# First group's softmax weights begun after half of its maxima, and q/k projections of the first batch placed between its up and down pieces

## The chip, the cores and the metric

The kernel runs on one core of one Trainium2 chip. The metric is the device time of one execution in microseconds. Engines are called as in the profile: PE (TensorE, with its weight loads PEld), DVE (VectorE), ACT (ScalarE), POOL (GpSimd) and SP (SyncE, here only an issuer of DMAs).

## The reference

A gated transformer block on x of shape 8 x 1024 x 256. Everything starts from the normalised input; attention and a feed-forward gate are multiplied and added to x.

```python
xn = _layernorm(x)
q, k, v = split(xn @ W_attn + b_attn)        # 16 heads of 16
q, k = _apply_rope(q), _apply_rope(k)
att = softmax(where(causal, q @ k.T / sqrt(16), -inf))
s = (att @ v) @ W_proj + b_proj
h = silu(xn @ (w_gate/127).T) * (xn @ (w_up/127).T)   # 768 hidden
g = silu(h @ (w_down/127).T)
out = x + s * g
```

## The kernel before

**Groups and steps.** The work is cut into 8 batches of 4 groups; a group is 4 heads of one batch. Queries and keys are halves of 512 and tiles of 128. For every group two things are done on the scores.

*Maxima.* `Group.maxima` (L499) computes scores with queries on the partitions, into one of three PSUM tiles `pm`, and DVE reduces them: `top_far` (L513) for keys of the first half seen by queries of the second, `trash`/`top` (L515) for the half on the diagonal. `maxima_units` lists 38 such units per group: 11 for the first half of the queries and 27 for the second (16 far ones of 512 columns, 11 on the diagonal). The maxima of one half are then split in two on POOL (`shift_parts`, L527), transposed on PE, copied to `rows` on ACT and written by two DMAs on SP into two rows of `q_st` (`shift_queries`, L537).

*Weights.* `Group.weights` (L552) computes the scores again with keys on the partitions into `pw`, now with the shift included through those rows of `q_st`, and ACT takes the exponential (L569). POOL clears the part above the diagonal (L576). `values` (L590) multiplies by v into `av`. There are 12 steps `n` per group (4 for the first half of the queries, 8 for the second) and 4 slots per step.

**The pipeline.** `attention` (L660) runs the weights of one group and, dealt over its 48 slots by `quarter_steps`, the maxima of the next group. In each slot, `slot` also runs pieces from one long list `chain`: projections of q, k and v (`project_qk`, `project_v`), the up pieces (`hidden`) and down pieces (`down`) of the feed-forward, output projections and transposes. The list is run by a pace: so much of it per slot that it ends with the batch. All instructions are in the order of the program on each engine; `manual_schedule` leaves it alone.

**The opening.** The first group has no group before it, so its maxima stand alone ahead of the first `attention`, with one piece of the chain after every other unit:

```python
for n, unit in enumerate(units):
    first.maxima(*unit)
    cast()
    if n % 2:
        run(1)
    if n in (8, 11, 14, 17):
        ...
        groups[1].load(which % 2, which // 2)
```

**q and k through DRAM.** `project_qk` leaves a pair `high`, `low` in SBUF (two buffers each), and SP stores both to a DRAM tensor `qk` (L254, 256 KB each). `Group.load` (L477) reads them back per group, head by head, into `q_st` and `k_st`: for each of q and k and each half four DMAs of 128 KB, each into 16 partitions (L483). All of these, the input x of the next batch (L87) and the rows of the shift (L544) go through SP's one queue in the order of the program.

**The lists.** For the first batch the chain begins with `qk[4:]` (q and k of the heads of groups 2 and 3), `v[2:]` and the 12 up pieces of the first quarter, then the 4 down pieces of that quarter. A down piece needs all gated products `h_high`, `h_low` that POOL makes from the up pieces.

Of the kernel before, what the change touches and what calls it, by code (L numbers as in the profile page):

```python
# [35 lines left out]
def gated_block_kernel(ctx: ExitStack, tc: tile.TileContext, x, wqk, wv, bv, wp, bp, wg, wu, wd, rope, out):  # L36
# [7 lines left out]
    QT = HALF // P  # L44
# [19 lines left out]
    def flush(keep=0):  # L64
        while len(later) > keep:
            later.pop(0)()

    def cast(keep=0):
        while len(casts) > keep:
            casts.pop(0)()  # L70
# [556 lines left out]
    STEPS = 3 * QT  # L627
# [3 lines left out]
    def add_values(count):  # L631
        for _ in range(count):
            of, half, kb, es = waiting.pop(0)
            ending = of.values(half, kb, es)
            if ending:
                endings.append(ending)

    def streams(columns, passes=1):
        return columns * passes / 2.4e3

    def quarter_steps(group, after):

        units = after.maxima_units() if after else []

        costs = [sum(0.2 + n / 960 for _ in heads) for _, heads, _, n in units]
        total, spent = sum(costs), 0.0
        plan = []
        for half, kb in group.weight_steps():
            columns = HALF - max(0, kb * P - half * HALF)
            for i in range(4):  # L650
                here = []
                while units and spent * 4 * STEPS < (len(plan) + 0.5) * total:
                    here.append(units.pop(0))
                    spent += costs.pop(0)
                weights = columns if 2 * columns > HALF else 2 * columns * (1 - i % 2)
                maxima = sum(len(heads) * max(n, 256) for _, heads, _, n in here)
                plan.append((streams(weights), streams(maxima), here))
        return plan

    def attention(groups, at, plan, slot, vector):  # L660

        group = groups[at]
        after = groups[at + 1] if at + 1 < len(groups) else None
        loaded = groups[at + 2] if at + 2 < len(groups) else None
        plan = iter(plan)
        for n, (half, kb) in enumerate(group.weight_steps()):
            es = []
            for pair in range(2):
                e, banks = group.weights(half, kb, pair)
                es.append(e)  # L670
                for second, bank in enumerate(banks):
                    weights, maxima, units = next(plan)
                    if bank:
                        bank()
                    cast()
                    slot(weights)
                    if pair == 0 and second and n == 2:
                        group.shift_queries(1)
                    if pair == 0 and second and n == QT + 3 and after:
                        after.shift_queries(0)  # L680
                    if pair == 1 and second and endings:
                        endings.pop(0)()
                    for unit in units:
                        after.maxima(*unit)
                    if not units:
                        flush()
                    slot(maxima)
                if vector:
                    vector.pop(0)()
            waiting.append((group, half, kb, es))  # L690
            if len(waiting) == 3:
                add_values(2)
            for entry in delayed:
                entry[0] -= 1
            while delayed and delayed[0][0] <= 0:
                delayed.pop(0)[1]()
            if n == QT - 1 and after:
                after.shift_parts(0)
            if n == STEPS - 1 and after:
                after.shift_parts(1)  # L700
            if loaded:
                if n == QT - 1:
                    loaded.load(0, 0)
                elif n == 2 * QT - 1:
                    loaded.load(1, 0)
                elif n == STEPS - 1:
                    loaded.load(0, 1)
                    loaded.load(1, 1)
# [14 lines left out]
    def forward(exact, general=None):  # L723
# [3 lines left out]
        groups = [None] * (NB * GROUPS)  # L727
# [12 lines left out]
        def by(count, pieces):  # L740
            return [pieces[i : i + count] for i in range(0, len(pieces), count)]

        def mixed(*kinds):
            both = [((i + 0.5) / len(x), p) for x in kinds for i, p in enumerate(x)]
            return [piece for _, pieces in sorted(both, key=lambda entry: entry[0]) for piece in pieces]

        qk, v = batches[0].project_in()
        chain = sum(qk[4:] + v[2:], [])
        aside = []
        marks = {}  # L750
        for b in range(NB):
            batches[b].weights, batches[b].general = weights, general
            last = b + 1 == NB

            outs = [[p[:1], p[1:]] for p in map(batches[b - 1].project, range(NT // 2))] if b else [[[], []]] * (NT // 2)
            (u0, d0), (u1, d1), (u2, d2), (u3, d3) = batches[b].feed_forward()
            (t0, o0), (t1, o1), (t2, o2), (t3, o3) = outs
            first = mixed(by(2, u0), aside)
            chain += first[:-2] + t0 + first[-2:]
            marks[b] = len(chain)  # L760

            if last:
                chain += o0 + d0[:2] + t1 + o1 + t2 + d0[2:] + o2 + t3 + u1
            else:
                chain += o0 + d0[:2] + t1 + d0[2:] + o1 + u1[:4] + t2 + u1[4:6] + o2 + u1[6:10] + t3 + u1[10:]
            chain += o3 + d1 + u2
            if last:
                chain += d2[:2] + u3[:6] + d2[2:] + u3[6:] + d3
                continue
            after = batches[b + 1]  # L770
            qk, v = after.project_in()
            if exact:
                chain += after.open() + d2 + mixed(by(2, u3), qk[:4]) + qk[4] + mixed(by(1, d3), by(1, after.splits()))
                aside = qk[5:] + v
            else:
                chain += d2 + u3 + after.open() + sum(qk[:4], []) + d3 + sum(qk[4:] + v, [])
# [13 lines left out]
        first = groups[0]  # L790
        for _, piece in batches[0].splits():
            piece()
        units = first.maxima_units()
        early = sum(qt < QT for qt, *_ in units)
        for n, unit in enumerate(units):
            first.maxima(*unit)
            cast()
            if n % 2:
                run(1)
            if n in (8, 11, 14, 17):  # L800
                which = (8, 11, 14, 17).index(n)
                groups[1].load(which % 2, which // 2)
            if n == early - 1:
                first.shift_parts(0)
            if n == early + 6:
                first.shift_queries(0)
        flush()
        first.shift_parts(1)
        for t in (wp_sb, bp_sb):
            nc.vector.tensor_scalar(t, t, QSCALE / 2, None, ALU.mult)  # L810

        for b in range(NB):

            here = range(b * GROUPS, (b + 1) * GROUPS)
            for i in here:
                open_group(groups, batches, i + 2)
            plans = [quarter_steps(groups[i], groups[i + 1] if i + 1 < len(groups) else None) for i in here]
            total = sum(w + m for plan in plans for w, m, _ in plan) + sum(us for us, _ in chain[done[0] : marks[b + 1]])
            slots = 2 * sum(len(plan) for plan in plans)
            due, spent, at = [0.0], [0.0], [0]  # L820
            vectors = []

            def slot(before):
                due[0] += total / slots
                spent[0] += before
                at[0] += 1
                while (
                    done[0] < (marks[b + 1] if b + 1 < NB or batches[b].complete[0] == GROUPS else marks[b + 1] - 6)
                    and spent[0] + chain[done[0]][0] / 2 <= due[0]
                ):  # L830
                    spent[0] += chain[done[0]][0]
                    run(1)
                if at[0] == 8 and b < NB - 1:
                    if b:
                        load_x(b + 1)
                    vectors.extend([lambda: None] * 5 + norm_steps(b + 1))

            for i, plan in zip(here, plans):
                attention(groups, i, plan, slot, vectors)
                groups[i] = None  # L840
            run(marks[b + 1] - done[0])
        while waiting:
# [12 lines left out]
    with tc.tile_pool(name="setup", bufs=1) as sp:  # L855
# [62 lines left out]
        early = Group(opening, 0)  # L918
        qk, v = opening.project_in()
# [82 lines left out]
```

## Time and profile before

| | us |
|---|---|
| median of 3 runs | 1567.24 (1566.38 to 1567.66) |
| the profiled execution | 1564.28 |
| its span | 1562.5 |
| busy of PE in the span | 1506.6 |
| busy of DVE | 1083.7 |
| busy of ACT | 958.6 |
| busy of POOL | 740.4 |
| mean granted PE clock | 0.994 |

The start of the profiled execution, as it stands in the timeline: the first maximum of the first group begins at 42.0 us, its first weights at 77.6 us; the last of its own maxima ends on DVE at 79.3 us; the first down piece begins at 85.0 us; the second group's weights begin at 129.0 us.

A page row of an engine gives busy time, its share of the span and the number of instructions. The slices cut the span in 40 parts of 39 us, and each digit is a busy share in tenths. In a list of waits the numbers are the total in us, how often, and the longest. In the windows an engine's number is its busy time in the stretch, with the count of its instructions in brackets; after the engines come the granted PE clock, the mean busy share of the 16 DMA engines, and GB/s. PE's busy time counts overlapping instructions once and includes their latency, so a busy PE is not a PE at full speed.

### The profile page before, as it was taken

To read this page: it belongs to the slowest core of one execution; us is meant where nothing else is said; L and a number is where in the kernel's file an instruction comes from. 1 tells how busy PE (TensorE), PEld (TensorE's weight loads), DVE (VectorE), ACT (ScalarE), POOL (GpSimd) and SP (SyncE) were. 2 spreads that over 40 slices of the span, in tenths; PEclk is the share of its full clock that TensorE was granted. 3 is DMA by queue.
4 is the path that set the end of the run, shared out by engine and by line. 5 is a ranking of instruction groups with operands and counts; after the bars stand their busy time and mean duration, and the time that the engine had idled before them with its cause. 6 is when DMAs were issued, how large, how long until landed. Compare 5 with 4: busy or idle time off the path is not lost.

```text
span 1562.5 us, 29525 instructions
## 1 busy us (share of the span) xinstructions
PE 1506.6 (96%) x9801; PEld 1057.9 (68%) x9801; DVE 1083.7 (69%) x3284; ACT 958.6 (61%) x2076; POOL 740.4 (47%) x1443
## 2 busy tenths in 40 slices
PE   5899999999999999999999999999999999999997
PEld 2567667776677766777667766777667776666664
DVE  6776766767767677776677766776776767777642
ACT  2157665676657666566665766667665766656664
POOL 4455443653436444464434734365353644434353
PEclk9899999999999999999999999999999999999999
DMA  6912544444554254643455454354454525445301
GB/s 178 193 29 42 110 96 62 96 63 96 110 96 75 36 123 91 107 72 59 100 86 105 66 96 96 70 101 63 95 110 89 82 37 123 84 75 83 49 16 44
DMA packets 92085, 132.86 MB, mean 85 GB/s; under 512 B 13713, under 2 KB 41873, under 8 KB 91922
## 3 DMA queue, kind: packets, MB, share of 16 engines
q1 hardware_dynamic: 90944, 129.82, 44.3%
q8 instruction: 80, 1.31, 0.4%
q10 hardware_dynamic: 978, 1.05, 0.3%
q14 instruction: 83, 0.68, 0.2%
HBM read 87.82 MB, written 41.94 MB: 83 GB/s over the span
## 4 chain that ended last, share of the span: by engine, by line
PE 85%; DVE 7%; ACT 2%; POOL 2%; DMA 1%; issue 1%; SPq 0%; ACTq 0%; DVEq 0%; POOLq 0%
PE pw L562 20%; PE av L598 17%; PE pm L504 17%; PE ph L325 10%; PE pqk L234 7%; PE pd L379 6%; PE pv L267 3%; PE po L432 3%; DVE top_far L513 2%; DVE trash L515 2%; ACT e L569 2%; PE py L616 1%; DVE st L103 1%; PE pyt L417 1%; DMA qk<-high 1%
## 5 line engine op out<-in xcount | busy, mean ns | idle before, releaser
L569 ACT ACTIVATE e<-pw 128x512 f32<-128x512 f32 (+2 forms) x1280 | 678.5, 558 | 415.1 <-PE pw L562 381.1
L515 DVE CUSTOM_DVE_ANT_0 trash<-pm,mask_q 128x128 bf16<-128x128 f32 (+3 forms) x1024 | 501.2, 490 | 314.2 <-PE pm L504 276.2
L562 PE MATMUL pw<-q_st,k_st 67*128 67x512 f32 (+3 forms) x1536 | 546.5, 389 | 7.6 <-ACT e L569 5.2
L504 PE MATMUL pm<-k_st,q_st 65*128 65x512 f32 (+3 forms) x1536 | 527.5, 382 | 9.6 <-DMA qk<-high 3.3
L562 PEld LDWEIGHTS pw<-q_st,k_st 67*128 67x128 f32 x1536 | 281.1, 189 | 202.5 <-issue 91.9
L576 POOL TENSOR_SCALAR_AFFINE_SELECT e<-e 128x256 f32<-128x256 f32 x512 | 206.3, 408 | 407.8 <-ACT e L569 406.7
L513 DVE TENSOR_REDUCE top_far<-pm 128x1 f32<-128x512 f32 x512 | 337.1, 684 | 57.7 <-PE pm L504 57.0
L504 PEld LDWEIGHTS pm<-k_st,q_st 65*128 65x128 f32 x1536 | 278.5, 191 | 73.2 <-DVE top L515 16.9
L598 PE MATMUL av<-e,v_sb 128*32 128x512 f32 (+3 forms) x3072 | 289.5, 494 | 0.3 <-POOL e L576 0.3
L356 POOL TENSOR_TENSOR th<-th,ups 128x256 f32<-128x256 f32 x192 | 140.5, 732 | 237.4 <-DVE th L352 232.8
L598 PEld LDWEIGHTS av<-e,v_sb 128*32 128x32 f32 x3072 | 80.5, 109 | 132.1 <-issue 98.9
L360 POOL TENSOR_TENSOR h_low<-th,h_high 128x256 fp32r<-128x256 f32 x192 | 140.8, 733 | 15.4
L234 PE MATMUL pqk<-xnT,wqk_sb 128*128 128x512 f32 x256 | 134.4, 611 | 0.3 <-DVE bqk_sb L912 0.3
L379 PE MATMUL pd<-wd_sb,h_high 128*128 128x256 f32 x384 | 98.0, 284 | 3.3 <-POOL h_high L359 3.3
L325 PE MATMUL ph<-xnT_high,wg_sb 128*128 128x256 f32 x384 | 100.4, 283 | 0.8 <-DVE th L352 0.8
L337 ACT ACTIVATE th<-ph 128x256 f32<-128x256 f32 x192 | 73.8, 385 | 42.6 <-PE ph L325 37.0
L325 PE MATMUL ph<-xnT_high,wu_sb 128*128 128x256 f32 x384 | 100.0, 282 | 0.0
L325 PE MATMUL ph<-xnT_low,wg_sb 128*128 128x256 f32 x384 | 99.2, 281 | 0.0
L325 PE MATMUL ph<-xnT_low,wu_sb 128*128 128x256 f32 x384 | 99.1, 280 | 0.0
L379 PE MATMUL pd<-wd_sb,h_low 128*128 128x256 f32 x384 | 97.3, 283 | 1.6 <-POOL h_low L360 1.6
L352 DVE SCALAR_TENSOR_TENSOR th<-th,ph 128x256 f32<-128x256 f32 x192 | 79.7, 415 | 18.5 <-ACT ups L341 17.0
L515 DVE DVE_READ_ACCUMULATOR2_ANT top<- 128x1 f32 x1024 | 85.1, 83 | 0.2 <-issue 0.2
(98 smaller groups left out, 1674.1 us busy)
## 6 DMA issues: line engine op xcount, KB each, us to landing
q_st<-qk SPq DMA_DIRECT2D x256, 128.0 KB, 4.1
k_st<-qk SPq DMA_DIRECT2D x256, 128.0 KB, 5.3
qk<-high SPq DMA_DIRECT2D x64, 256.0 KB, 3.0
qk<-low SPq DMA_DIRECT2D x64, 256.0 KB, 2.9
xs<-in_x SPq DMA_DIRECT2D x16, 512.0 KB, 8.4
res<-in_x SPq DMA_DIRECT2D x32, 256.0 KB, 4.9
out<-res SPq DMA_DIRECT2D x32, 256.0 KB, 2.5
q_st<-rows SPq DMA_DIRECT2D x128, 8.0 KB, 1.9
```

The source lines that it names most:

```text
L234: nc.tensor.matmul(pt, wqk_sb[:, c, ts(i, P)], xnT[:, c, ts(half, HALF)], start=(c == 0), stop=(c == CC - 1),)
L325: nc.tensor.matmul(pt, self.weights[up][:, c, ts(hc, P)], part[:, c, ts(quarter, QU)], start=(c == 0 and i == 0), stop=(c == CC - 1 and i ...
L356: nc.gpsimd.tensor_tensor(h, th, ups, ALU.mult)
L360: nc.gpsimd.tensor_tensor(low, th, high.bitcast(F32), ALU.subtract)
L379: nc.tensor.matmul(pt, h[:, ts(i, P)], self.weights[2][:, hc, :], start=(hc == 0 and n == 0), stop=(hc == HC - 1 and n == len(hs) - 1),)
L504: nc.tensor.matmul(pm[:, ts(i, n)], self.q_st[half][:SHIFT, head, at], self.k_st[keys][:SHIFT, head, :n], start=True, stop=True,)
L513: nc.vector.tensor_reduce(self.top_far[:, head, qt - QT : qt - QT + 1], pm, AX.X, ALU.max)
L515: nc.vector.tensor_tensor_reduce(trash[:, :n], pm[:, ts(i, n)], mask_q[:, HALF - n :], 1.0, MASKED, ALU.add, ALU.max, self.top[:, head, qt ...
L562: nc.tensor.matmul(pw[:, ts(i, n)], self.k_st[kb // QT][:, head, ts(kb % QT, P)], self.q_st[half][:, head, lo:], start=True, stop=True,)
L569: nc.scalar.activation(e[:, first : first + count, lo:], pw[:, : count * n].rearrange("p (a n) -> p a n", n=n), AF.Exp,)
L576: nc.gpsimd.affine_select(out=e[:, :, lo : lo + P], in_=e[:, :, lo : lo + P], pattern=[[0, 2], [1, P]], compare_op=ALU.is_ge, fill=0.0, ba ...
L598: nc.tensor.matmul(self.av[ts(j, SLOT), lo:], vs[self.batch.b % 2][:, kb, at : at + SLOT], es[j // 2][:, j % 2, lo:], start=(kb == 0), sto ...
```

## The change

**Opening.** Only the first 19 of the 38 units (all 11 of the first half of the queries, and 8 more) are run alone ahead of the first group. Two pieces of the chain are run per three units, 12 in all instead of 19. The loads of group 1 move from units 8, 11, 14, 17 to 5, 7, 9, 11, and `shift_queries(0)` from unit 17 to unit 14.

**First group.** The other 19 units (`own`) are dealt over its first 12 slots, steps 0 to 2, and the 38 units of group 1 over the remaining 36. `shift_parts(1)` of the first group comes at the end of step 2 and `shift_queries(1)` in step 3 instead of before the group and in step 2. For group 1, `shift_parts(0)` comes at the end of step 6 and `shift_queries(0)` in step 9, where they were in steps 3 and 7. Other groups keep their places; the sharing rule is written anew and deals the same units to their 48 slots.

**Chain of the first batch.** It begins with `v[2:]` and `qk[4:6]`, then the first quarter's up pieces, then `qk[6:]` (q and k of the second half of the positions), then the down pieces.

```diff
+    AHEAD = 4 * (QT - 1)
+
+    def quarter_steps(group, after, own):
+        def shares(of, units, begin, end):
+            costs = [sum(0.2 + n / 960 for _ in heads) for _, heads, _, n in units]
+            total, spent, dealt = sum(costs), 0.0, [[] for _ in range(4 * STEPS)]
+            for unit, cost in zip(units, costs):
+                at = begin + int(spent / total * (end - begin) + 0.5)
+                dealt[min(at, end - 1)].append((of, unit))
+                spent += cost
+            return dealt
+
+        first = shares(group, own, 0, AHEAD)
+        second = shares(after, after.maxima_units() if after else [], AHEAD if own else 0, 4 * STEPS)
...
-                    if pair == 0 and second and n == 2:
+                    if pair == 0 and second and n == (QT - 1 if own else 2):
                         group.shift_queries(1)
-                    if pair == 0 and second and n == QT + 3 and after:
+                    if pair == 0 and second and n == (2 * QT + 1 if own else QT + 3) and after:
                         after.shift_queries(0)
...
-                    for unit in units:
-                        after.maxima(*unit)
+                    for of, unit in units:
+                        of.maxima(*unit)
...
-            if n == QT - 1 and after:
+            if n == QT - 2 and own:
+                group.shift_parts(1)
+            if n == QT - 1 and after and not own or n == 2 * QT - 2 and own:
                 after.shift_parts(0)
...
-        chain = sum(qk[4:] + v[2:], [])
+        chain = sum(v[2:] + qk[4:6], [])
...
-            first = mixed(by(2, u0), aside)
-            chain += first[:-2] + t0 + first[-2:]
+            if b == 0:
+                chain += u0 + sum(qk[6:], [])
+            else:
+                first = mixed(by(2, u0), aside)
+                chain += first[:-2] + t0 + first[-2:]
...
-        for n, unit in enumerate(units):
+        own = units[early + 8 :]
+        for n, unit in enumerate(units[: early + 8]):
             first.maxima(*unit)
             cast()
-            if n % 2:
+            if n % 3:
                 run(1)
-            if n in (8, 11, 14, 17):
-                which = (8, 11, 14, 17).index(n)
+            if n in (5, 7, 9, 11):
+                which = (5, 7, 9, 11).index(n)
                 groups[1].load(which % 2, which // 2)
             if n == early - 1:
                 first.shift_parts(0)
-            if n == early + 6:
+            if n == early + 3:
                 first.shift_queries(0)
         flush()
-        first.shift_parts(1)
```

More of the change, by code (lines that the diff above doesn't have):

```diff
@@ L639, in streams @@
         return columns * passes / 2.4e3
[L641 to L646, printed above, removed]
+    AHEAD = 4 * (QT - 1)
[10 more added lines that the diff above has]
+        second = shares(after, after.maxima_units() if after else [], AHEAD if own else 0, 4 * STEPS)
         plan = []
@@ L650, in quarter_steps, with attention @@
             for i in range(4):
[L651 to L654, printed above, removed]
+                here = first[len(plan)] + second[len(plan)]
                 weights = columns if 2 * columns > HALF else 2 * columns * (1 - i % 2)
-                maxima = sum(len(heads) * max(n, 256) for _, heads, _, n in here)
+                maxima = sum(len(heads) * max(n, 256) for _, (_, heads, _, n) in here)
                 plan.append((streams(weights), streams(maxima), here))
         return plan
-    def attention(groups, at, plan, slot, vector):
+    def attention(groups, at, plan, slot, vector, own):
         group = groups[at]
@@ L816, in forward @@
                 open_group(groups, batches, i + 2)
-            plans = [quarter_steps(groups[i], groups[i + 1] if i + 1 < len(groups) else None) for i in here]
+            plans = [
+                quarter_steps(groups[i], groups[i + 1] if i + 1 < len(groups) else None, [] if i else own) for i in here
+            ]
             total = sum(w + m for plan in plans for w, m, _ in plan) + sum(us for us, _ in chain[done[0] : marks[b + 1]])
@@ L838, in forward @@
             for i, plan in zip(here, plans):
-                attention(groups, i, plan, slot, vectors)
+                attention(groups, i, plan, slot, vectors, not i)
                 groups[i] = None
```

## The prediction

> **What bounds the kernel now.** I read four views in this order. The page first: TensorE (PE) is the busiest engine by far, so over most of the span only work on PE, or a wait of PE, moves the end.
>
> ```profile
> PE 1506.6 (96%) x9801; PEld 1057.9 (68%) x9801; DVE 1083.7 (69%) x3284; ACT 958.6 (61%) x2076; POOL 740.4 (47%) x1443
> PE   5899999999999999999999999999999999999997
> ```
>
> The slices below 9 are the first two, so what the change can win or lose lies before about 130 us. Second, PE's waits there, by window (42 to 78 us, then 78 to 130 us):
>
> ```profile
> PE pm L504 <- DMA qk<-high: 3.3, 1, 3.3
> PE pm L504 <- DVE top_far L513: 2.5, 2, 2.2
> PE pm L504 <- DVE top L515: 0.8, 3, 0.3
> ...
> PE pd L379 <- POOL h_high L359: 2.8, 2, 1.5
> PE pd L379 <- POOL h_low L360: 1.1, 3, 0.4
> ```
>
> The 3.3 us is before the first maximum and stays. The 2.5 us is a chain: ACT waited 6.6 us for a `high` buffer whose store had not landed. The `pd` waits are the down pieces that come right behind the last up piece. Third, the timeline around the rows of the queries' shifts:
>
> ```profile
> 61.67 0.26 ACT L542 COPY rows<-pq 32x128 f32<-32x128 f32 x1 [3.20 <-PE pq L540]
> 66.28 0.34 SPq L254 DMA_DIRECT2D qk<-high  x1
> 66.71 0.38 SPq L254 DMA_DIRECT2D qk<-low  x1
> 67.14 2.29 SPq L483 DMA_DIRECT2D k_st<-qk  x4
> 69.82 17.61 SPq L544 DMA_DIRECT2D q_st<-rows  x4
> 77.59 0.40 PE L562 MATMUL pw<-q_st,k_st 67*128 67x512 f32 x1
> ```
>
> The rows are ready on ACT at 61.9 us, but their transfer is issued at 69.8 us, behind everything else in SP's queue, and lands 4.9 us later (the DMA view of that issue), at 74.7. The first `pw`, which needs them, comes at 77.6, so nobody waits. Fourth, the windows (busy of PE, PEld, DVE, ACT, POOL, clock, DMA share, GB/s) tell why the queue is late:
>
> ```profile
> 44.00:52.00 8.00, 7.70 (x21) 3.84 (x20) 6.90 (x25) 1.38 (x2) 7.94 (x6) 0.87 1.09 130
> 52.00:55.00 3.00, 2.66 (x8) 1.09 (x7) 2.53 (x7) 0.00 (x0) 2.37 (x4) 1.00 1.09 341
> 55.00:58.00 3.00, 1.43 (x7) 0.60 (x5) 0.73 (x2) 0.90 (x2) 0.00 (x0) 1.00 1.08 382
> 58.00:66.00 8.00, 6.88 (x19) 4.94 (x20) 6.05 (x19) 0.73 (x2) 0.00 (x0) 0.61 1.08 160
> 66.00:75.00 9.00, 8.36 (x41) 6.30 (x39) 8.68 (x24) 1.32 (x4) 1.86 (x3) 0.97 0.78 188
> ```
>
> The DMA share is full without a gap from 44 to about 72 us. 44 to 52 moves 1.04 MB, which is the eight 128 KB head loads issued at 42.2 to 46.2; 52 to 58 moves 2.2 MB, the next batch's x (1 MB) and four stores (1 MB). So head loads run at about 130 GB/s, stores and x at 340 to 400. The opening is bound by DVE on one side and by this backlog on the other.
>
> **The change part by part.** *Opening: 19 units instead of 38, 12 pieces instead of 19.* DVE sets its pace. In before DVE ran units 0 to 10 from 42.8 to 53.4 with two `low` operations (0.75 each) among them; now two `v_sb` (0.68) and one `low` stand there: 54.0. Then seven far maxima at 0.64, one unit of four at 1.2, one `low`, two `th` (0.42): 7.3 us, so 61.3. PE issues its last maximum two tiles ahead and reaches the first `pw` at about **60 us** (77.6 before). The 2.5 us wait is gone, because only two q/k tiles are projected here and both find a free `high` buffer. The scaling of wp and bp on DVE (0.41 + 0.48) costs nothing as long as PE then waits; without that wait it would delay DVE by 0.9.
>
> *What PE finds there: the rows.* `shift_queries(0)` moves from unit 17 to unit 14, its PE transpose, ACT copy and two DMAs with it, and the 16 loads of group 1 from units 8 to 17 to units 5 to 11. On SP's queue, though, the rows still stand behind the x, behind all 16 loads, and behind the stores of `qk[4]` and `qk[5]`. Only the four stores of `qk[6:]` are now behind them. Issuing loads earlier wins nothing where the DMA share is already full. Four stores of 256 KB at 382 GB/s are 2.7 us: the rows land at 74.7 - 2.7 = **72 us**. PE is in order, and the first maximum of the group's own second half stands behind that `pw`: all of PE waits about **12 us**. Bounds: 69.5, if loads overlap the stores better; 74.7, if the stores were hidden under the loads.
>
> A rule of the Trainium skill says otherwise: "DMA: Bandwidth & Descriptors", section "Bandwidth", measures 341 GB/s for a 1 MB transfer from HBM into 128 partitions. By it the queue from 52 us on (x 1.05 MB, loads 2.1, four stores 1.05) takes 12.3 us, the rows land at about 64 and the wait is 4 us; the whole sum below would then end near zero (+0.8). But each of these loads fills only 16 partitions, and the row at 44 to 52 shows 130 GB/s with nothing else moving. The trace decides.
>
> *Slots 0 to 11 of the first group.* A step has four slots. By the new sharing they hold 19 own units, 12 banks of weights and four `hidden` pieces. PE restarts at half clock. The trace shows 0.50 from 60 to 66 us behind an idle stretch of only 2.3 us; "TensorE: Matmul & The Clock Gate", "What's actually happening", gives about 3.4 us of busy time at half clock. In slots 0 to 3 PE has 2.9 us of work at full clock, 5.7 at half, against 3.9 us on DVE. I take 5 (4.6 by the page, 5.7 by the trace): 77 us. Slots 4 to 11 are DVE's: 6 far at 0.64, four of 384 columns at 0.71, four of 512 at 0.84 (distance of successive starts in the timeline), two `th`: 10.9 us, so 88. Then the shift of half 1: DVE 0.21, POOL 0.20 + 0.22 but behind a gate product (0.73 + 0.40 + 0.73) or a diagonal select (0.41) in POOL's queue: 89. Transpose, ACT copy 0.26 behind exponentials, two issues of 0.57 and a landing of 1.9 (the page's median): 92.2. PE has only about 1.7 us to do between slots 13 and 16, so it waits again for POOL, then for the rows (3 to 4 us in all); queued behind are the exponentials and all later maxima. Before, this shift stood in slot 9, its operands long ready. Slot 16 begins at **92.2**.
>
> *Same work in before.* At slot 9, 84.97 us, before had done the same own units and all up pieces. Against this, after at slot 16 has more: three further banks of weights (0.75) and two steps of values (16 `av`, 1.6 at full clock); and less: four q/k pieces (0.9 each) and four maxima of 384 columns (0.18 each): 2.0 us less. So it stands where before stood at 83.0: behind by **9.2 us**.
>
> *Up, then q/k, then down.* Before loses at the two down groups 2.2 us (87 to 90.2), 1.7 by the clock of 0.54 in the following 3.7 us, and 1.8 at 121 us: 5.7. The first is removed, since d0 now comes at slot 30. But the delay moves on: in group 1 the last up piece of the second quarter now falls in slot 7 and its down pieces in slots 9 to 10, among diagonal selects on POOL, as d0 did: 3.3 us expected again. Gain **2.4** (ends 0 and 5.7).
>
> *Slots 16 to 47.* Group 1's 38 units now share 36 slots, not 48. In slots 16 to 30 DVE has 12.6 us of maxima, 4.5 of the next batch's statistics (0.42 + 0.18 each), two `low` and a finish: 19; PE has about 15 to 16. Three maxima tiles let DVE lag by about 2 us. Cost **2** (0 to 4). After that PE leads again. `shift_queries(0)` of group 1 moves to slot 37, 11 slots ahead of its use: nothing. Group 2's loads in half 1 need the q/k pieces of slots 16 to 27 and come after slot 47: nothing. The total of pieces and units is unchanged, so nothing is given back later.
>
> Sum: +9.2 - 2.4 + 2 = **+8.8 us** on the profiled execution's 1564.28. That execution is 2.96 below the median of the runs shown (1567.24), so the median forecast is 1567.24 + 8.8 = 1576.0.
>
> **The rivals.**
> 1. *The rows stall PE* (the sum): 1571 to 1583, 0.67.
> 2. *The backlog clears early, and the change wins.* One mechanism: the rows' landing. If the loads, now in one unbroken run, went at the stores' speed, the rows would land by about 61 and the 12 us wait falls to 1: 8.8 - 11 = -2.2, and with the down stall of group 1 (3.3) gone too, -5.5: 1562 to 1565. It decides at a landing of about 63 us. For it: the mixed stretch 66 to 75 moved 188 GB/s. Against: 130 and 160 in the load stretches. 0.12.
> 3. *Half of each*: rows at 66 to 68 (8.8 - 5), the down stalls gone: 0 to +3, about 1568.5. 0.12.
> 4. *DVE becomes the bound for the whole first group* (57 units in 48 slots, 43 us of maxima at the page's durations) on top of the stall: +13 to +18, about 1582.5. Against: in 94 to 126 DVE was 24.5 of 32 us busy with 25 to 28 units. 0.09.
>
> That the change does not do what it says belongs to case 1: in program order the weights begin behind the first half's maxima, in time they begin with the transfer.
>
> **How the numbers follow.** A measurement of this kernel can tell about 0.2%, 3.1 us. Case 2 is faster in most of it (0.1); the rest of it and case 3 give 0.14 within; the rest, 0.76, is slower. The range 1566.5 to 1583 leaves out case 2 and the far end of case 4, under 2 in 10.
>
> **What would show it.** Right: a wait of `pw` L562 on DMA near 60 to 72 us of about 12 us, the clock at 0.5 behind it; DMA share full to 72; a shorter wait of PE at the shift of half 1 near 89 to 92; no `pd` wait in group 0 but one in group 1; own maxima ending on DVE near 88 (79.3 before). Wrong: the first `pw` running before 65 us, or the last load landing before 62.

## The result and the profile after

The changed kernel is slower, by 0.6%. Its median is 1574.03 us over 8 runs (1572.06 to 1575.41) against 1566.14 for the kernel before in the same series (8 runs, 1560.0 to 1568.36); the ratio is 1.0062, 95% interval 1.0047 to 1.0077. The forecast was 1576.0. The profiled executions lie further apart, 1575.31 and 1564.28, because that of the changed kernel is near the top of its runs. The 67 runs of the kernel before that stand beside the experiments have medians near 1564.4 us; against them the change costs 9.6 us instead of 7.9.

PE's waits between 42 and 100 us and then from 135 to 150 us, where before had 2.5 us of `pm` on DVE and 3.9 us of `pd`:

```profile
PE pw L562 <- DMA q_st<-rows: 14.5, 2, 13.2
PE pm L504 <- DMA qk<-high: 3.6, 1, 3.6
PE pm L504 <- ACT rows L542: 0.8, 1, 0.8
...
PE pd L379 <- POOL h_high L359: 1.2, 1, 1.2
PE pd L379 <- POOL h_low L360: 0.4, 1, 0.4
```

The first line is new. SP's queue in the timeline (start, duration, what is issued) and the first weights on PE show where it stands:

```profile
48.11 2.28 SPq L483 DMA_DIRECT2D q_st<-qk  x4
51.34 5.24 SPq L483 DMA_DIRECT2D k_st<-qk  x4
57.05 0.34 SPq L254 DMA_DIRECT2D qk<-high  x1
57.95 0.34 SPq L254 DMA_DIRECT2D qk<-low  x1
58.82 3.50 SPq L483 DMA_DIRECT2D q_st<-qk  x4
62.84 2.09 SPq L483 DMA_DIRECT2D k_st<-qk  x4
65.52 0.34 SPq L254 DMA_DIRECT2D qk<-high  x1
66.41 0.34 SPq L254 DMA_DIRECT2D qk<-low  x1
67.29 28.75 SPq L544 DMA_DIRECT2D q_st<-rows  x4
73.52 0.77 PE L562 MATMUL pw<-q_st,k_st 67*128 67x512 f32 x1 [13.24 <-DMA q_st<-rows]
```

The loads begin at 48.1 us instead of 52.5, as the change wants, but each group of four takes up to 5.2 us to issue, and the rows leave at 67.3, only 2.5 us earlier than before. PE was ready at 60.3. The windows of this stretch (PE, PEld, DVE, ACT, POOL busy, clock, DMA share, GB/s):

```profile
60.00:66.00 6.00, 0.28 (x1) 0.00 (x0) 3.24 (x7) 0.55 (x2) 3.81 (x6) 0.68 1.08 212
66.00:73.50 7.50, 0.00 (x0) 0.01 (x1) 0.00 (x0) 0.00 (x0) 0.00 (x0) 0.50 0.75 138
73.50:80.00 6.50, 6.48 (x22) 5.73 (x23) 3.62 (x11) 2.95 (x7) 0.81 (x2) 0.50 0.00 0
80.00:92.00 12.00, 12.00 (x45) 8.62 (x47) 9.49 (x25) 3.81 (x9) 5.62 (x12) 0.50 0.00 0
92.00:98.00 6.00, 4.73 (x36) 3.45 (x29) 3.22 (x16) 2.26 (x8) 2.15 (x5) 0.93 0.11 35
```

All compute engines stand still from 66 to 73.5 us. Behind it PE is busy without a gap to 92 us, but at half clock, and DVE, which should have set the pace there, is busy for only 13.1 of 18.5 us. PE itself sets the pace: from its first weights to 92 us it waits for no other engine, and the 256-column matmuls of the up pieces start 0.21 us apart (74.5 to 75.2 us), where at full clock they start 0.12 us apart (58.5 to 58.9 us).

Where the time goes is seen in the starts of the groups' first weights in the two timelines. Group 0 begins 4.1 us earlier than before (73.5 against 77.6), group 1 begins 5.1 later (134.1, 129.0), group 4, the first of the second batch, 12.3 later:

```profile
266.15 0.40 PE L562 MATMUL pw<-q_st,k_st 67*128 67x512 f32 x1
...
278.47 0.40 PE L562 MATMUL pw<-q_st,k_st 67*128 67x512 f32 x1
```

The first line is before, the second after. From there on the distance stays at 12.2 to 12.8 us to the last group. Groups 1 to 3 add 7.2 us. They run pieces that were not run in the opening and in group 0: about 30 more matmuls of up pieces and 24 more of down pieces than before, some 6.5 us by an estimate at 0.12 us each. The `pd` wait of group 1 adds to it.

### The profile page after: what moved, and what is told of

It is laid out like the page before. It is cut to its first block, busy times and chain, and to the rows that moved or that the text cites. A ratio compares the mean times of both kernels' runs of the same rounds, so it can differ in the third digit from the quotient of the medians.

```text
span 1573.6 us, 29511 instructions
## 1 busy us (share of the span) xinstructions
PE 1510.7 (96%) x9801; PEld 1064.9 (68%) x9801; DVE 1084.0 (69%) x3284; ACT 959.0 (61%) x2076; POOL 740.5 (47%) x1443
## 4 chain that ended last, share of the span: by engine, by line
PE 84%; DVE 7%; ACT 2%; DMA 1%; POOL 1%; issue 1%; DVEq 0%; ACTq 0%; POOLq 0%
PE pw L562 19%; PE av L598 17%; PE pm L504 17%; PE ph L325 10%; PE pqk L234 6%; PE pd L379 6%; PE pv L267 3%; PE po L432 3%; DVE trash L515 2%; DVE top_far L513 2%; ACT e L569 2%; PE py L616 1%; PE pyt L417 1%; DVE st L103 1%; PE pxt L225 1%
```

## The experiments

All ratios are to the kernel before, run on the same chip in the same series (median 1564.45 of 39 runs for the first four, 1564.38 of 28 for the last four).

**1. Loads behind the rows.** On the changed kernel:

```diff
-            if n in (5, 7, 9, 11):
-                which = (5, 7, 9, 11).index(n)
+            if n in (15, 16, 17, 18):
+                which = (15, 16, 17, 18).index(n)
```

> The changed kernel with the four loads of group 1 issued at units 15 to 18 of the opening, behind shift_queries(0), instead of at units 5 to 11. Theory (the rows of the shift stand behind 2 MB of head loads in the DMA backlog): the rows land near 60 to 62 us instead of 73.5, the wait of pw on q_st<-rows falls from 13.2 us to under 2, the clock does not stay at 0.5 behind it, and with the slower slots gone too the time falls by 13 to 17 us, to 1557 to 1561. Rival (57 units of maxima in the first group's 48 slots make DVE the bound): the wait goes but comes back as waits of pm on DVE in slots 0 to 30; 1569 to 1574.

Measured: 1560.43 us, ratio 0.997 (0.9959 to 0.9981), 13.6 us under the changed kernel. The rows now leave at 58.7 us, ahead of all 16 loads, and the first weights begin at 61.3. PE's waits from 42 to 270 us no longer have the 13 us; the windows that follow are the surprise:

```profile
PE pw L562 <- DMA q_st<-rows: 1.3, 1, 1.3
...
66.00:73.50 7.50, 7.50 (x28) 6.39 (x27) 6.14 (x18) 3.71 (x10) 3.45 (x7) 0.55 1.09 122
73.50:80.00 6.50, 6.50 (x28) 3.22 (x27) 5.10 (x13) 0.91 (x3) 2.65 (x6) 0.50 0.65 73
```

The wait and what hangs on it is the loss: with it removed the change is a gain of 0.3%. But the clock falls to half without any long wait: from 43 to 67 us, behind the wait at the first maximum, the longest is 1.3 us. So the half clock is not a consequence of the 13 us alone. (The trace is of the slowest of the 11 runs, 1562.83 us.)

**2. The rows on ACT's queue.** On the changed kernel:

```diff
-                nc.sync.dma_start(
+                (nc.scalar if self.name == "0_0" and half == 0 else nc.sync).dma_start(
                     out=self.q_st[half][SHIFT + r : SHIFT + r + 1, :, :].bitcast(F32),
```

> The changed kernel with only the two DMAs of the first group's first shift issued from ACT's queue instead of SP's; all loads keep their place on SP. Theory A (it is the order within SP's queue): the rows land 2 to 3 us behind ACT's copy, near 60 to 62 us, the wait falls to under 2 us, 1557 to 1562. Theory B (the 16 DMA engines are full, whoever issues): the rows still wait for packets of the loads ahead of them, the wait of pw stays over 8 us, 1570 to 1575.

Measured: 1567.99 us, ratio 1.0018 (1.0008 to 1.0029), between the theories. In the profiled execution ACT issues at 56.6 to 58.2 us and the first weights begin at 62.8:

```profile
56.33 0.24 ACT L542 COPY rows<-pq 32x128 f32<-32x128 f32 x1
56.60 1.58 ACTq L544 DMA_DIRECT2D q_st<-rows  x2
...
62.79 0.62 PE L562 MATMUL pw<-q_st,k_st 67*128 67x512 f32 x1 [3.61 <-DMA q_st<-rows]
```

So most of the 13 us was the place in SP's queue, and another queue passes it; 3.6 us remain while the engines are full of loads. That execution (1563.49) is among the three quickest of 20; the three lie below 1564 us, the other 17 between 1566.7 and 1570.6, so the trace does not speak for most of them. The mean granted clock of the 17 is 0.983 to 0.988, that of the three 0.987 to 0.990, so more half clock is part of it; what brings it stays open.

**3. PE kept busy while it waits.** On the changed kernel:

```diff
         flush()
+        warm = fill_tile("warm")
+        for _ in range(14):
+            nc.tensor.matmul(warm, wqk_sb[:, 0, :P], xnT[:, 0, :HALF], start=True, stop=True)
```

> The changed kernel with 14 matmuls of 512 fp32 columns, whose result nobody reads, put on PE between the opening and the first group (about 12 us at full clock), so that PE is busy while the rows are on their way. Theory (the half clock from 73 to 92 us, not only the wait, costs time): the rows land as before near 73, the clock is 1.0 from there, slots 0 to 15 take about 19 us instead of 24, and the time falls by 4 to 5 us to 1569 to 1571. Rival (in these slots DVE sets the pace, the clock costs nothing): 1573 to 1576.

Measured: 1572.03 us, ratio 1.004 (1.0027 to 1.0054), about 2 us under the changed kernel, with intervals that overlap. In the trace slots 0 to 15 take 21.3 us instead of 23.9 (from the first `pw` at 74.0 to the first of step 4 at 95.3). Two windows of this kernel say why it is not more:

```profile
73.50:80.00 6.50, 5.72 (x27) 4.05 (x28) 4.82 (x14) 3.81 (x8) 1.28 (x4) 1.00 0.00 0
80.00:92.00 12.00, 12.00 (x54) 7.96 (x52) 8.20 (x23) 3.36 (x8) 5.36 (x12) 0.57 0.00 1
```

The clock is whole to 80 us and then falls anyway. A warm PE at the start of this stretch buys 2.7 us there, not the 4 to 5 expected.

**4. The order of the chain alone.** On the kernel before:

```diff
-        chain = sum(qk[4:] + v[2:], [])
+        chain = sum(v[2:] + qk[4:6], [])
...
+            if b == 0:
+                chain += u0 + sum(qk[6:], [])
```

> The kernel before with only the new order of the first batch's chain (v[2:], qk[4:6], up pieces, qk[6:], then down pieces); opening, sharing and loads as before. Theory: the order is a gain by itself: the 2.5 us wait of pm at 56 us (behind a high buffer) goes, and the wait of the first down pieces (2.2 us and 1.7 us of slow clock) moves or goes: 2 to 5 us under before, 1561 to 1564. Rival (the order is what costs, because its stores and down pieces come late): 1568 or more.

Measured: 1557.49 us, ratio 0.9941 (0.9917 to 0.9965), more than expected. Its waits from 80 to 135 us:

```profile
PE pd L379 <- POOL h_high L359: 0.8, 1, 0.8
PE pw L562 <- ACT e L569: 0.5, 2, 0.3
PE pd L379 <- POOL h_low L360: 0.4, 1, 0.4
```

Its first weights begin at 74.1 us (77.6 before), group 1 at 121.5 (129.0). So 3.5 us come from the opening, where no q/k tile waits for a `high` buffer and the half clock of 60 to 66 us is gone, and 4.0 from group 0, where the first quarter's down pieces no longer wait; the 1.2 us of `pd` left are the second quarter's, at 118 us. At the start of the second batch 6.5 of the 7.5 us are left (259.7 against 266.2).

**5. The sharing alone.** The changed kernel with the old chain:

```diff
-        chain = sum(v[2:] + qk[4:6], [])
+        chain = sum(qk[4:] + v[2:], [])
...
-            if b == 0:
-                chain += u0 + sum(qk[6:], [])
```

> The changed kernel with the old order of the first batch's chain (qk[4:], v[2:], up and then down pieces), so only the opening, the sharing and the places of the loads and shifts are new. Theory (the rows' transfer sets when the first weights begin, and four more stores of 256 KB stand ahead of it): the rows land 2.5 to 3 us later than in the changed kernel, near 76, the wait of the old down pieces (about 4 us with the clock) is back, the time is 4 to 7 us over the changed kernel: 1577 to 1581. If the two parts simply add (the changed order alone was 7.0 us under before), it is 1581. Rival (the order of the chain is what keeps the changed kernel slow): under 1570.

Measured: 1572.32 us, ratio 1.0054 (1.0036 to 1.0071): not slower than the changed kernel. Expectation and addition both fail, and so does the rival, which asked for under 1570. PE's waits, 42 to 85 us and then 85 to 270 us:

```profile
PE pw L562 <- DMA q_st<-rows: 6.9, 1, 6.9
PE pm L504 <- DVE top L515: 5.6, 1, 5.6
...
PE pd L379 <- POOL h_low L360: 0.4, 1, 0.4
PE pd L379 <- POOL h_high L359: 0.2, 1, 0.2
```

The opening waits 5.6 us by the old order (2.5 in the kernel before), but PE then waits that much less for the rows: the first weights begin at 72.7 us. And the rows do not land later for four more stores ahead of them: from the first load of the half-1 heads (40.95, in the changed kernel 42.03) to the first weights it is 31.8 us, there 31.5. So in the changed kernel the chain's order bought nothing: what it saved in the opening went into the wait. Nor did it save `pd` waits: with the old order they are 0.6 us, in the changed kernel 1.6 with a stretch of half clock behind them. Group 1 takes 47.1 us here and 50.0 there.

**6. Half of the loads behind the rows.** As 1, with units `(5, 7, 15, 16)`.

> The changed kernel with two of the four loads of group 1 (eight DMAs, 1 MB) moved behind the rows, to units 15 and 16; the other two keep units 5 and 7. Theory (the wait is the bytes of head loads ahead of the rows): half the loads, half the way: the rows land near 67 us, the wait is 6 to 8 us, the time 1565 to 1569, between 1574.0 with all loads ahead and 1560.4 with none. Rival (a threshold, or the place of the shift itself): the wait stays over 11 us or goes to under 2.

Measured: 1567.61 us, ratio 1.0016 (1.0008 to 1.0024). The wait as expected:

```profile
PE pw L562 <- DMA q_st<-rows: 7.3, 1, 7.3
```

First weights at 61.3, 66.4 and 73.5 us with none, half and all of the loads ahead go with 1560.4, 1567.6 and 1574.0 us. The more bytes of loads stand ahead of the rows, the longer the time; the three points show no threshold.

**7. Fewer units shared.** As 1, with the following edit. It also runs 18 pieces of the chain in the opening instead of 12, since the loop over the units runs two pieces for every three:

```diff
-        own = units[early + 8 :]
-        for n, unit in enumerate(units[: early + 8]):
+        own = units[early + 16 :]
+        for n, unit in enumerate(units[: early + 16]):
```

> As e1_loads_behind (loads behind the rows), but 27 units are run in the opening and 11 are left for the first group's first 12 slots, instead of 19 and 19. Theory (what sharing costs by itself, some 3 us against the changed order alone, is the stretch in which DVE sets PE's pace and the clock stays at 0.5): with fewer units dealt there the stretch of 0.5 gets shorter and the time is 1 to 3 us under e1_loads_behind, 1557.5 to 1559.5. Rival (sharing itself is neutral): the same as e1_loads_behind within 1 us.

Measured: 1558.74 us, ratio 0.9959 (0.9944 to 0.9973). The direction is the expected one, but the interval overlaps that of the first experiment. Its windows:

```profile
66.00:73.50 7.50, 7.47 (x32) 6.11 (x33) 6.36 (x17) 3.77 (x9) 5.78 (x11) 0.77 1.09 122
73.50:80.00 6.50, 6.50 (x36) 3.29 (x35) 5.43 (x14) 3.37 (x7) 3.59 (x8) 1.00 0.78 142
```

The clock is whole from 73.5 to 80 us (0.78 from 80 to 92), and slots 0 to 15 take 17.7 us (23.7 in experiment 1). But they begin 7.0 us later, at 68.3, because the opening is longer: slot 16 begins at 86.0 us, in experiment 1 at 85.1. With six more pieces run in the opening, the gain can't be put down to the clock alone.

**8. One q/k group behind each of the first two quarters' up pieces.** On the kernel of experiment 4:

```diff
-                chain += u0 + sum(qk[6:], [])
+                chain += u0 + qk[6]
+                u1 = u1 + qk[7]
```

> As e4_chain_only (before, with only the new order of the first batch's chain), but qk[7] goes between the second quarter's up and down pieces instead of in front of the first quarter's down pieces, where qk[6] stays. Theory (each pair of q/k pieces between up and down covers one wait of pd on POOL): the pd wait of the second quarter, 1.2 us in e4_chain_only, goes, that of the first does not come back over 0.5 us, and the time is 1 to 2 us under 1557.5. Rival (two pieces do not cover it): 1557 to 1560.

Measured: 1554.42 us, ratio 0.9938 (0.9918 to 0.9958), the best of all, though its interval doesn't separate it from experiment 4. Its waits of PE from 85 to 270 us are one line, none of `pd`:

```profile
PE pw L562 <- ACT e L569: 2.1, 7, 0.6
```

The second batch begins at 257.3 us (259.7 in experiment 4, 266.2 before). Of the 2.4 us against experiment 4, 1.5 are already there at the first weights (72.6 against 74.1), up to which PE runs the same work in the same order in both, so that part is spread; 0.9 come in group 0, where the `pd` wait was.

## Why the prediction was right, point by point

- **Arrival of PE at the first weights**: 60 predicted, 60.3 measured (73.52 less the wait of 13.24).
- **Landing of the rows**: 72 predicted, 73.5 measured; the wait 12 and 13.2. The term that was off is the 2.7 us credited for four stores moved behind the rows. Experiment 5, which puts them ahead again, needs only 0.3 us more from the first load to the first weights; the bound named for "stores hidden under the loads", 74.7, was the nearer one. The rate of the head loads held: 130 GB/s in the kernel before, 122 in experiment 1 with loads alone (66 to 73.5 us). The 341 GB/s that the Trainium skill measures for 128 partitions ("DMA: Bandwidth & Descriptors", "Bandwidth") would have put the wait at 4 us, 9 too short.
- **The half clock** was the term most under-sized, and the pace of the stretch was given to the wrong engine. The prediction took 5 us for slots 0 to 3 and then let DVE set the pace of slots 4 to 11. The trace has 0.50 for all of 73.5 to 92 us, and PE sets the pace. The own maxima ended on DVE at 91.3 (88 predicted), slot 16 began at 97.45 (92.2). The rule of the Trainium skill that the prediction cites, about 3.4 us of busy time ("TensorE: Matmul & The Clock Gate", "What's actually happening"), is off by a factor of five here: PE was busy for 18.48 us at 0.50. Experiments 1 and 3 show that the idle stretch isn't needed for it: the clock falls in this stretch also when PE comes to it without one. What makes it fall there and stay low, no run here shows.
- **The shift of the second half**: 3 to 4 us of waiting predicted, 1.3 measured, because PE at half clock reached the transpose (94.26) after the split was done (92.06).
- **Up, q/k, down**: no `pd` wait in group 0 and one in group 1, as predicted: 1.6 us, and a clock of 0.50 from 147.5 to 150.9 us. By an estimate that loses 3.3 us (1.6, and half of 3.4) and leaves the predicted gain of 2.4 on the 5.7 of before. But the cause named for it, the order of the chain, is wrong: experiment 5 keeps the old order and has only 0.6 us of `pd` wait, so the rest of the change takes the old wait away, and the new order brings one back. The step also missed that the same order is worth 7 us where nothing else stands in front of the weights (experiment 4); the prediction's sum had its opening part in the arrival at 60, where the wait swallowed it.
- **Slots 16 to 47** took 36.7 us (97.45 to 134.1), in the kernel before 32.2 (96.8 to 129.0). The prediction put 2 us, 0 to 4, on the maxima that are crowded into them. The two stretches do not hold the same pieces of the chain, so the 4.5 us do not measure that term.
- **The sum**: +8.8 predicted, +7.9 by the medians of the first series (+9.6 against the later ones), +12.3 in the two profiled executions by the start of the second batch. Part of the difference between these is spread of the runs. The close hit is partly luck: with the 5.2 us that slot 16 came later than predicted, the prediction's own sum would be 14.0 where the traces have 12.3, so its other terms were about 1.7 too dear in all. Which of them is not shown. The wait that decides the sign, and the queue that makes it, were forecast as they came.
- **The rivals**: the second one, the early landing, priced the kernel without the wait at 2.2 to 5.5 us under before. Experiment 1, which takes the wait away by another road, is 4.0 under.

## What to carry to other kernels

Before moving a consumer earlier, find the transfer it needs and count what stands ahead of it in its queue: issuing bulk loads earlier into DMA engines that are already full only puts them in front of the small urgent one. Put the urgent transfer first, or leave the consumer where its data arrive. A saving upstream of such a wait is worth nothing until the wait is gone, so the parts of a change are best timed apart: here the order of the chain alone gains 0.6%, and the sharing with the loads as placed turns that into a loss. Nor does any run show that the sharing itself gains: with the loads behind the rows it gives 1560.4 us (1558.7 with fewer units shared), the order without it 1557.5, with intervals that overlap.

## What the hardware showed that was not expected

PE's granted clock stayed at 0.50 from 73.5 to 92 us of the changed kernel while the profile has PE busy for 18.48 of these 18.5 us, and in experiment 1 it fell to half near 67 us behind no wait of more than 1.3 us. Loads of 128 KB into 16 partitions ran at 122 and 130 GB/s with a DMA share of 1.09, where the windows of stores and x had 341 and 382; four more stores among such loads, 1 MB, lengthened the queue by 0.3 us (experiment 5 against the changed kernel, one trace of each).
